# Moving the outer left sums of layer 0 to VectorE, ordering a logarithm behind a copy, and taking the last quad's inner sums from one quad earlier, in a two-layer graph kernel

## The chip, the cores and the metric

The kernel runs on one core of one Trainium2 chip. The metric is the device time of one execution in microseconds (us). All data are 32-bit floats. TensorE multiplies matrices, VectorE, ScalarE and GpSimd do the elementwise work, and the queues of SyncE, GpSimd and ScalarE start the transfers. In the lines of the profile these are PE (with PEld for its weight loads), DVE, ACT, POOL and SP.

## The reference

There are 128 graphs of 128 nodes with 512 features. Each of two layers normalises the features, applies a ReLU, runs a graph layer and adds the result to its input.

```python
# layer 0
h = maximum(layernorm(x), 0)
Xw = h @ Wv + bv
e = leaky_relu((Xw @ aw[:d])[:, None, :] + (Xw @ aw[d:])[:, :, None] + ab, 0.2)
a = adj * exp(e)
T = a / (sum(a, -1) + 1e-12)
x1 = x + relu(h @ Wk[0] + bk[0] + T @ h @ Wk[1] + bk[1] + T @ T @ h @ Wk[2] + bk[2])
# layer 1
h2 = maximum(layernorm(x1), 0)
q, k = split(h2 @ Wqk)
w = sum(q * (adj @ (k * mask)), -1) * mask / sqrt(512)
out = x1 + softmax(w, over the nodes)[:, :, None] * (h2 @ Wv1)
```

## The kernel before, in words

**Pairs and quads.** Layer 0 walks over 64 pairs of graphs, `for p in range(NP)`. Layer 1 walks over 32 quads, each two pairs, `q` from 0 to `NQ - 1`. All large products are done by a seven-product scheme of the Strassen-Winograd kind: the operands are cut into blocks, some sums of blocks are formed beforehand (the left sums of the activations, the right sums of the weights), and seven products replace eight. The results are chained through four PSUM banks `a`, `b`, `c`, `e`: after product 1 into `a`, ScalarE copies `a` to `b`; after product 6 has accumulated into `b`, ScalarE copies `b` to `c` (line 380, the value called U2 in Winograd's scheme); product 7 accumulates into `c`; ScalarE copies that to a buffer `s` (line 384); product 4 accumulates into `c` again. So product 7 waits for the copy of line 380, and product 4 for the copy of line 384. TensorE takes its instructions in the order written.

**One pair of layer 0.** The loop body for pair p runs: the attention matrix of pair p (`attention`, lines 454 to 473: scores z, an exponential, a row sum, the normalised matrix t, and beside it the transposed adjacency aT, scaled by the node mask on ScalarE in line 472); the products `y10` of pair p in the banks set1, with the transposes of t after product 6; `for_layer1(p - 1)`; the small products `inner` and `outer` with t; the sum with x in `outer` (line 526, VectorE); the products `y2` of pair p + 2 in the banks set2; two copies that seed the banks of the next `y10` (lines 486 and 490, after line 526); and `norm2(p)`, the layer norm of the result for layer 1. `norm0(p + 3)` and `begin(p + 2)` (norm, transposes in line 336 and left sums in lines 352 to 355 of later pairs) run in the course of `y10`.

**A layer norm.** `statistics` takes mean and variance on VectorE (lines 280 and 281), then a logarithm and an exponential on ScalarE (lines 285 and 286, the inverse root), five small VectorE instructions, and `norm_relu` applies the result with two large ScalarE instructions (line 304). The result goes to DRAM and comes back by 32x32 blocks, so that VectorE can transpose it.

**The outer left sums.** Layer 1 uses the seven-product scheme twice, one inside the other. `for_layer1(p)` transposes four blocks of a pair (line 410). After every second pair it forms the four outer left sums of the quad (lines 418, 419, 421, 422) and writes them to DRAM in two transfers of 1024 KB (lines 420 and 423). These sums are done by GpSimd for all quads but the last, which VectorE does.

**One quad of layer 1.** Two rounds of seven products run in step in the two sets of banks. Before the products, the inner left sums of each factor are formed from the outer ones, four VectorE instructions for the first four factors (called EARLY) and four for the other three (LATE: 3, 7, 4). The first round of an ordinary quad uses the factors 1, 5, 2, 6, the second 3, 7, 4. The last quad has another order: its first round uses 1, 6 and 2, 7, so it needs a LATE factor from its second product on. `scores` forms the row scores of the quad before (lines listed as `junk<-agg,wscale,c`), `spread_scores` sends them through DRAM to all partitions (`pwd`, `pw`), and `peaks` takes their maximum when they are back, ahead of the softmax.

**What sets the order.** A scheduler lays out each engine's instructions by priority (the order in which they are written) and by when it expects their inputs. `behind(what, op, ...)` fixes an order on top of it: `op` comes after the instruction `done[what]` on the engine that both run on. It adds nothing where the two run on different engines: `done["warm"]` is a matmul, so it holds back nothing on ScalarE. In layer 1 the orders are written out by hand: `dve`, `act`, `pool` and `sync` put each instruction behind the one before.

Of the kernel before, what the change touches and what calls it, by code (L numbers as in the profile page):

```python
# [8 lines left out]
FP = mybir.dt.float32  # L9
# [6 lines left out]
def kernel(  # L16
# [25 lines left out]
    nc = tc.nc  # L42
    B, N, D = x.shape
    K = wk.shape[0]
    P = 128
# [52 lines left out]
    def load_x(p, queue=nc.sync):  # L98
        xg[p] = loads.tile([P, G, D], FP, name="xg")
        queue.dma_start(xg[p], x[p * G:(p + 1) * G].rearrange("b n d -> n b d"))  # L100
# [78 lines left out]
    for dst, w in weights0:  # L179
        rows(dst, w, range(HC))  # L180

# [93 lines left out]
    def statistics(src):  # L275
# [9 lines left out]
        nc.scalar.activation(r[:, 0], var, AF.Ln, bias=eps)  # L285
# [73 lines left out]
    def strassen(banks, left, right, s, first, ends, steps={}, gate="warm"):  # L359
# [20 lines left out]
        nc.scalar.copy(c, b)  # L380
# [20 lines left out]
    def for_layer1(p):  # L401
# [10 lines left out]
        if second:  # L412
            fv = FW.pop(q).rearrange("p o j k n -> p o (j k n)")
            fd = FD[q].rearrange("p o j k n -> p o (j k n)")
            at = {o: fv[:, i] for o, i in SLOT.items()}

            engine, queue = (nc.gpsimd, nc.gpsimd) if q + 1 < NQ else (nc.vector, nc.sync)
            engine.tensor_add(at[5], fv[:, L21], at[4])
            engine.tensor_sub(at[6], at[5], at[1])
            queue.dma_start(fd[:, :4].rearrange("p o n -> p (o n)"), fv[:, :4].rearrange("p o n -> p (o n)"))  # L420
            engine.tensor_sub(at[3], at[2], at[6])
            engine.tensor_sub(at[7], at[1], fv[:, L21])  # L422
            queue.dma_start(fd[:, 4:].rearrange("p o n -> p (o n)"), fv[:, 4:].rearrange("p o n -> p (o n)"))
# [25 lines left out]
    def attention(p):  # L449
# [20 lines left out]
        for j in range(G):  # L470
            b = p * G + j
            nc.scalar.activation(aT[:, j, :], aT[:, j, :], AF.Copy, scale=maskT[:, b:b + 1])
# [57 lines left out]
    def norm2(p):  # L530

        HV2[p] = by_blocks(norm_relu(X1[p]), H2D[p])
# [45 lines left out]
    def inner_sums(q, factors):  # L578
# [3 lines left out]
        s = early.tile([P, 4, n, N], FP, name=f"in{first}")  # L582
# [37 lines left out]
    with tc.issue_after(done["hv"]):  # L620
        for p in (2, 3):
            load_x(p)
        load_adj(2)
        rows(rl[:, :, 1], wv1)

    for p in range(NP):
# [27 lines left out]
        behind("left", outer, p, z)  # L654
# [242 lines left out]
    for q in range(NQ - 1):  # L897
# [29 lines left out]
        if q > 0:  # L927
# [6 lines left out]
                     6: [lambda: scale(prior, 0, 1)]}  # L934
        together(one_round(q, set1, (3, 7), s1, adding_ends(lambda i, j: c[:, 0::3, i, j],
# [17 lines left out]
    for step in inner_sums(q, LATE):  # L953
        step()
# [113 lines left out]
```

## Time and profile before

The time before is 2357.18 us, the median of three runs (2349.5 to 2360.67). The profiled execution spans 2351.3 us. Layer 0 takes the first 1545 us or so, layer 1 the rest.

| stretch of the profile, us | PE busy | DVE busy | ACT busy | POOL busy |
|---|---|---|---|---|
| 0 to 100 (start of layer 0) | 85.12 | 52.80 | 39.39 | 20.22 |
| 300 to 600 (layer 0) | 286.60 | 195.89 | 151.35 | 86.28 |
| 900 to 1200 (layer 0) | 294.56 | 202.37 | 157.93 | 90.26 |
| 2000 to 2300 (layer 1) | 296.33 | 242.52 | 185.54 | 161.60 |
| 2300 to 2352 (end) | 32.89 | 36.48 | 21.67 | 11.07 |

A line of the timeline gives the start, the duration, the engine, the line of the kernel, the operation, the tiles written and read with their shapes, and how many instructions were merged (x4). Brackets give the idle time of that engine just before, and what released it. A line of the waits gives who waited for whom, the sum, the number of times and the longest, in us. A line of the stretches gives the busy time and the number of merged instructions of each engine, then TensorE's granted clock, the share of the DMA engines and the rate.

### The profile page before, as it was taken

The page shows a single profiled execution, that of the slowest core. Times are in us where ns is not written, and L with a number is a line of the kernel's source. Part 1 is how long each engine was busy: PE and PEld are TensorE (multiplying, and loading weights), DVE is VectorE, ACT ScalarE, POOL GpSimd, SP SyncE. Part 2 cuts the span into 40 slices and gives each one's busy share as a digit, 9 for nine tenths or more (in the row PEclk, how much of TensorE's full clock was granted, in tenths as well). Part 3 has the DMA queues.
Part 4 walks back from the last instruction along what each step waited for, and adds up shares of the span by engine and source line. Part 5 has one row for each costly group of instructions (what it writes and reads, how often), then busy time and mean ns, then how long its engine had stood idle before and what let it go on. Part 6 is the DMA issues. An engine that isn't in the chain of part 4 may idle for free.

```text
span 2351.3 us, 28892 instructions
## 1 busy us (share of the span) xinstructions
PE 2259.5 (96%) x8227; PEld 1541.8 (66%) x8227; DVE 1669.9 (71%) x4342; ACT 1262.1 (54%) x2932; POOL 847.4 (36%) x911
## 2 busy tenths in 40 slices
PE   8899999999999999999999999999999999999996
PEld 5565555656656566565665656578877878888785
DVE  5576665767667676676766667578877788888786
ACT  3444444555555455555555555446656666666564
POOL 2132222322322232232232223245545555555552
PEclk9999999999999999999999999999999999999998
DMA  7577686666676666666667666668787888888786
GB/s 212 154 233 231 203 248 197 216 216 209 194 235 201 199 228 201 206 211 215 205 205 224 198 198 225 203 240 238 225 226 228 223 239 233 222 238 239 219 233 166
DMA packets 343502, 507.77 MB, mean 216 GB/s; under 512 B 33178, under 2 KB 198426, under 8 KB 326958
## 3 DMA queue, kind: packets, MB, share of 16 engines
q1 hardware_dynamic: 302060, 382.40, 51.8%
q0 software_dynamic: 40992, 123.00, 19.7%
q8 instruction: 65, 1.06, 0.2%
q14 instruction: 95, 0.78, 0.1%
q10 hardware_dynamic: 290, 0.53, 0.1%
HBM read 289.62 MB, written 216.18 MB: 215 GB/s over the span
## 4 chain that ended last, share of the span: by engine, by line
PE 64%; DVE 16%; DMA 11%; ACT 4%; issue 3%; POOL 1%; SPq 1%; DVEq 0%; ACTq 0%
PE c L90 19%; PE a L90 18%; PE b L90 17%; PE e L90 10%; DMA pw<-pwd 3%; DVE junk L553 3%; DMA xg<-in_x_dram 2%; DVE x L526 2%; DVE st L280 2%; DMA pwd<-pwt 2%; ACT h L304 1%; DVE c L553 1%; DMA h2d<-h 1%; DVE s L553 1%; DVE in L553 1%
## 5 line engine op out<-in xcount | busy, mean ns | idle before, releaser
L553 POOL TENSOR_TENSOR c<-s,c 128x512 f32<-128x512 f32 (+1 forms) x186 | 199.9, 1089 | 370.4 <-DVE s L553 365.6
L110 POOL DMA_DIRECT2D agb<-in_adj_dram x256 | 150.3, 592 | 431.5 <-DVE aT L468 331.8
L90 PE MATMUL a<-r,x 128*128 128x512 f32 x512 | 246.4, 604 | 0.8 <-ACT a L486 0.5
L553 DVE SCALAR_TENSOR_TENSOR junk<-agg,wscale,c 128x512 f32<-128x512 f32 x128 | 197.6, 1543 | 31.7 <-POOL c L553 25.8
L90 PE MATMUL b<-rw,in 128*128 128x256 f32 x896 | 217.2, 382 | 0.9 <-ACT b L553 0.9
L90 PEld LDWEIGHTS b<-rw,in 128*128 128x128 f32 x896 | 172.0, 192 | 25.1 <-ACT b L553 1.3
L85 DVE TENSOR_TENSOR e<-e,s 128x512 f32<-128x512 f32 x64 | 44.7, 699 | 184.9 <-ACT s L384 184.9
L553 POOL TENSOR_TENSOR c<-c 128x1024 f32<-128x1024 f32 x62 | 159.5, 2573 | 2.8 <-DVE c L553 0.4
L90 PEld LDWEIGHTS a<-r,x 128*128 128x128 f32 x512 | 94.3, 195 | 68.2 <-issue 63.8
L90 PE MATMUL a<-w,x 128*128 128x257 f32 x512 | 131.9, 380 | 2.8 <-DVE z L454 2.8
L90 PE MATMUL b<-t,sx 128*128 128x512 f32 x256 | 124.3, 609 | 9.3 <-ACT b L376 9.3
L90 PE MATMUL b<-w,sx 128*128 128x257 f32 x512 | 132.1, 380 | 0.8 <-ACT b L376 0.6
L553 ACT ACTIVATE c<-c,wcol 128x512 f32<-128x512 f32 x124 | 86.2, 720 | 79.6 <-DVE wcol L553 79.6
L422 POOL TENSOR_TENSOR fw<-fw 128x512 f32<-128x512 f32 x31 | 39.1, 1263 | 247.7 <-DVE fw L410 247.7
L280 DVE BATCH_NORM_STATS2 st<-xg 128x6 f32<-128x512 f32 x128 | 82.1, 683 | 64.4 <-DMA xg<-in_x_dram 64.4
L90 PE MATMUL c<-t,x 128*128 128x512 f32 x256 | 120.9, 595 | 4.3 <-ACT s L384 4.3
L90 PE MATMUL c<-rw,in 128*128 128x256 f32 x448 | 110.1, 385 | 13.3 <-ACT c L553 13.1
L376 ACT COPY b<-a 128x257 f32<-128x257 f32 (+1 forms) x128 | 59.4, 464 | 116.5 <-PE a L90 116.3
L90 PE MATMUL e<-t,sx 128*128 128x512 f32 x256 | 120.3, 592 | 0.0
L90 PE MATMUL c<-t,sx 128*128 128x512 f32 x256 | 120.3, 592 | 0.0
L90 PE MATMUL b<-r,sx 128*128 128x512 f32 x256 | 120.3, 592 | 0.0
L90 PE MATMUL e<-rw,in 128*128 128x256 f32 x448 | 108.5, 381 | 5.8 <-DVE in L553 5.5
(247 smaller groups left out, 5351.3 us busy)
## 6 DMA issues: line engine op xcount, KB each, us to landing
fd<-fw POOLq DMA_DIRECT2D x62, 1024.0 KB, 6.6
x1d<-x SPq DMA_DIRECT2D x64, 512.0 KB, 2.8
h2d<-h SPq DMA_DIRECT2D x64, 512.0 KB, 4.8
hv<-h2d SPq DMA_DIRECT2D x256, 128.0 KB, 3.5
f<-fd SPq DMA_DIRECT2D x32, 1024.0 KB, 9.6
xg<-in_x_dram SPq DMA_DIRECT2D x63, 512.0 KB, 5.1
hd<-h SPq DMA_DIRECT2D x63, 512.0 KB, 3.1
hv<-hd SPq DMA_DIRECT2D x252, 128.0 KB, 2.9
```

The costliest lines, as they stand in the source:

```text
L85: return op(*args, **how)
L90: done["mm"] = op(*args, **how).ins
L110: nc.gpsimd.dma_start(agb[p][c * S32:(c + 1) * S32].rearrange("p g q i -> p (g q) i"), v[c])
L280: nc.vector.bn_stats(st, src[:, j, :])
L304: nc.scalar.activation(to, at, AF.Relu, bias=rs[:, 1, j:j + 1], scale=rs[:, 0, j:j + 1])
L376: nc.scalar.copy(b, a)
L422: engine.tensor_sub(at[7], at[1], fv[:, L21])
L526: done["x1"] = nc.vector.scalar_tensor_tensor(hb[:, j, at], bank[:, HD:], 0.0, xs[:, j, at], OP.max, OP.add).ins
L553: done[engine] = op(*args, **how).ins
```

## The change

There are four edits.

1. The four outer left sums of every quad are done by VectorE, right behind the transposes whose results they add, and before the sums with x (line 526), which are put behind the last of them. The transfers stay on GpSimd's queue.
2. The logarithm of `norm2` (line 285) is put behind the copy of U2 (line 380) in the `y2` just issued, the copy of U2 behind the copy of line 85, and the scaling of the transposed adjacency (line 472) behind the exponential of line 456.
3. The four LATE inner sums of the last quad move from that quad's start into the second round of the quad before, in buffers of their own.
4. The input of pair 2 is loaded at the start, behind the weights, and no longer after pair 1's first norm.

```diff
     for dst, w in weights0:
         rows(dst, w, range(HC))
+    load_x(2)
...
-    def statistics(src):
+    def statistics(src, gate="warm"):
...
-        nc.scalar.activation(r[:, 0], var, AF.Ln, bias=eps)
+        behind(gate, nc.scalar.activation, r[:, 0], var, AF.Ln, bias=eps)
...
         product(b, 6)
-        nc.scalar.copy(c, b)
+        done["u2"] = behind("s", nc.scalar.copy, c, b).ins
...
-            engine, queue = (nc.gpsimd, nc.gpsimd) if q + 1 < NQ else (nc.vector, nc.sync)
-            engine.tensor_add(at[5], fv[:, L21], at[4])
-            engine.tensor_sub(at[6], at[5], at[1])
+            queue = nc.gpsimd if q + 1 < NQ else nc.sync
+            nc.vector.tensor_add(at[5], fv[:, L21], at[4])
+            nc.vector.tensor_sub(at[6], at[5], at[1])
             queue.dma_start(fd[:, :4].rearrange("p o n -> p (o n)"), fv[:, :4].rearrange("p o n -> p (o n)"))
-            engine.tensor_sub(at[3], at[2], at[6])
-            engine.tensor_sub(at[7], at[1], fv[:, L21])
+            nc.vector.tensor_sub(at[7], at[1], fv[:, L21])
+            done["c12"] = nc.vector.tensor_sub(at[3], at[2], at[6]).ins
...
-            nc.scalar.activation(aT[:, j, :], aT[:, j, :], AF.Copy, scale=maskT[:, b:b + 1])
+            behind("z", nc.scalar.activation, aT[:, j, :], aT[:, j, :], AF.Copy, scale=maskT[:, b:b + 1])
...
-        HV2[p] = by_blocks(norm_relu(X1[p]), H2D[p])
+        HV2[p] = by_blocks(norm_relu(X1[p], rs=statistics(X1[p], "u2")), H2D[p])
...
-    def inner_sums(q, factors):
+    def inner_sums(q, factors, space=None):
...
-        s = early.tile([P, 4, n, N], FP, name=f"in{first}")
+        s = (space or early).tile([P, 4, n, N], FP, name=f"in{first}")
...
-        for p in (2, 3):
-            load_x(p)
+        load_x(3)
...
-        behind("left", outer, p, z)
+        behind("c12" if p else "left", outer, p, z)
...
+        if q == NQ - 2:
+            sums = inner_sums(NQ - 1, LATE, back[3])
+            hooks[2], hooks[3] = hooks[2] + sums[:2], hooks[3] + sums[2:]
...
-    for step in inner_sums(q, LATE):
-        step()
```

## The prediction

> **What bounds the kernel now.** I read the stretches first, then the waits of TensorE, then the timeline where these waits lie. A settled stretch of layer 0 and one of layer 1:
>
> ```profile
> 600.00:900.00 300.00, 294.25 (x989) 182.19 (x988) 205.16 (x663) 158.44 (x377) 87.16 (x121) 1.00 0.68 214
> ...
> 2000.00:2300.00 300.00, 296.33 (x1266) 240.89 (x1265) 242.52 (x419) 185.54 (x419) 161.60 (x120) 0.99 0.82 232
> ```
>
> TensorE (first number) is busy 98% of both stages, so it sets the pace, and only what makes it wait can be won: under 6 us in 300. TensorE's waits in 600 to 900 say what that is:
>
> ```profile
> PE c L90 <- ACT c L380: 5.1, 7, 0.7
> ...
> PE c L90 <- ACT s L384: 0.7, 1, 0.7
> ```
>
> Seven times in 300 us, once in two pairs (a double pair takes 45.0 us). Over the whole trace this wait is 17.8 us in 24 times. The timeline of such a pair:
>
> ```profile
> 600.13 1.28 POOL L421 TENSOR_TENSOR fw<-fw 128x512 f32<-128x512 f32 x1
> ...
> 600.40 1.10 DVE L454 TENSOR_SCALAR z<-pz,y,cz 128x128 f32<-128x128 f32 x1
> ...
> 601.63 0.29 ACT L285 ACTIVATE r<-mv,eps 128x2 f32<-128x2 f32 x1 [0.74 <-DVE mv L281]
> ...
> 602.22 0.40 ACT L472 ACTIVATE aT<-aT,maskT 128x128 f32<-128x128 f32 x1
> ...
> 602.52 0.36 ACT L380 COPY c<-b 128x257 f32<-128x257 f32 x1
> ...
> 602.94 1.13 PE L90 MATMUL c<-w,sx 128*128 128x257 f32 x4 [0.72 <-ACT c L380]
> ...
> 623.29 0.32 DVE L454 TENSOR_SCALAR z<-pz,y,cz 128x128 f32<-128x128 f32 x1
> ```
>
> The z instruction takes 1.10 us while GpSimd adds, and 0.32 in the next pair, where GpSimd has no sums. The variance behind it comes late, ScalarE sits 0.74 us before the logarithm, and U2's copy, queued behind logarithm, exponential and mask scaling, starts at 602.52, though product 6 was over at 601.35. TensorE stands for 0.72 us.
>
> Before 400 us the loss is larger. An early pair with sums:
>
> ```profile
> 169.97 0.36 ACT L380 COPY c<-b 128x257 f32<-128x257 f32 x1 [0.49 <-PE b L90]
> ...
> 171.80 0.30 ACT L285 ACTIVATE r<-mv,eps 128x2 f32<-128x2 f32 x1 [1.47 <-DVE mv L281]
> ...
> 172.36 0.36 ACT L384 COPY s<-c 128x257 f32<-128x257 f32 x1
> ...
> 173.34 1.71 DVE L454 TENSOR_SCALAR z<-pz,y,cz 128x128 f32<-128x128 f32 x1
> ...
> 177.35 1.52 ACT L304 ACTIVATE h<-x,rs 128x512 f32<-128x512 f32 x2
> ...
> 179.99 3.43 PE L90 MATMUL b<-t,sx 128*128 128x512 f32 x4 [2.65 <-ACT b L376]
> ```
>
> VectorE is held up by GpSimd's adds (two sums of `prepare` took 1.38 and 1.40 us, in the pair after 0.39 each), so z and norm are late, ScalarE's copy of line 376 is queued behind them, and TensorE waits 2.65 us and runs at half clock afterwards (3.43 us for what takes 1.88). Between 100 and 395 us such waits add up to 19.5 us (0.79, 2.65, 2.65, 3.80, 1.18, 0.92, 2.39, 3.83, 1.32).
>
> At the start the second pair waits for the input of pair 2, at the end the last quad for its LATE sums:
>
> ```profile
> 51.10 1.29 DVE L280 BATCH_NORM_STATS2 st<-xg 128x6 f32<-128x512 f32 x2 [4.06 <-DMA xg<-in_x_dram]
> ...
> 68.69 1.13 PE L90 MATMUL a<-w,x 128*128 128x257 f32 x4 [2.82 <-DVE z L454]
> ```
>
> ```profile
> 2312.61 1.22 PE L90 MATMUL e<-rw,in 128*128 128x256 f32 x2 [5.48 <-DVE in L553]
> ...
> 2313.62 3.62 PE L90 MATMUL b<-rw,in 128*128 128x256 f32 x8
> ...
> 2322.74 0.68 DVE L553 TENSOR_REDUCE peak<-pw 128x4 f32<-128x512 f32 x1
> ...
> 2327.71 0.70 PE L90 MATMUL a<-rw,f 128*128 128x256 f32 x2
> ```
>
> **What the Trainium skill says.** "SBUF — State Buffer", section "Who interferes with whom": VectorE and GpSimd share a port pair under an exclusive lock; a VectorE instruction with two SBUF inputs, or a `tensor_scalar` in its two-port mode, waits for the whole of a GpSimd instruction that reads SBUF. The trace agrees: 1.10 and 1.71 us against 0.32. "TensorE: Matmul & The Clock Gate", section "What's actually happening": after an idle window of about 3.4 us the clock halves until TensorE has been busy as long. The trace agrees in kind: after 5.5 us of idling eight matmuls took 3.62 us, against 1.89 in other rounds; here 2.65 us was enough too, and 0.72 never was.
>
> **The sums on VectorE.** They leave GpSimd (31 quads of four, 1.26 to 1.28 us each), which has time enough, so the time saved there is worth nothing by itself. On VectorE the same shape took 0.65 to 0.68 us in the last quad, started every 0.57 to 0.60: 4 x 0.6, and 0.1 for a dependence, make 2.5 us a quad, 78 us over layer 0, where VectorE is busy 68%. In a settled pair the transposes start at 594.23; 1.36 us later come the sums, so line 526 can start at 598.1, and started at 597.49. It is 0.6 us late, and behind it queue the seed copies: 598.55 and 599.07, free at 599.65, when the next copy (line 376) started before: 599.65. So the delay just fits, and TensorE sees at most 0.1. Later VectorE has 4.00 us of idle time (before 592.57) to catch up in. The two 1024 KB transfers start 2 to 3 us earlier on a queue that nothing waits for here. What is won: z costs 0.32 for 1.10.
>
> **Logarithm behind U2's copy.** No instruction is added. The copy can start at 601.4 and ends at 601.8, before TensorE is through with product 2 (602.22): the 0.72 us is gone. New is that logarithm, exponential, five small VectorE instructions and the two large ones of line 304 queue behind the copy. In the pairs without sums the logarithm moves from 623.73 to about 624.6 and line 304 from 625.78 to 626.6. Their result goes to DRAM and has 10 us until it is transposed. The mask scaling behind the exponential gives the exponential its place 0.4 us sooner; the scaled matrix is first read in layer 1.
> Sum for the settled part: 24 x 0.72 = 17.3 us, less 24 x 0.1 for the late seeds and about 1 us for other small waits: -14.
>
> **Early pairs.** VectorE gets back 1.0 + 1.0 + 1.4 = 3.4 us of blocking for 2.5 us of sums, but the sums and the transposes must now come before line 526. There the transposes stood behind it (167.72 against 166.08); VectorE was idle for 2.28 us before it, so line 526 comes between 1.6 us (4 - 2.3, if the blocks are there) and 4 us later. That puts up to 1 us on U2's chain and takes some 2 us off the chain z, norm, line 376. I take half of the 19.5 us: -9; the bounds are 0 and -19.5 with up to 1.5 us of slow clock for each of four waits.
>
> **Input of pair 2.** The load is on the queue behind the weights, with the DMA engines full from 10 to 30 us, so it lands at 30 us or so instead of 51. What goes before it isn't moved. The 4.06 us wait of VectorE goes, TensorE's 2.82 us with it, as TensorE was free at 65.9. With 0.5 us for the exponential of pair 0 that now precedes the mask scaling: -3. Bounds: 0 and -6.
>
> **LATE sums.** Four instructions of 0.55 us leave the gap in which TensorE stood 5.48 us and lost another 2.3 us to half clock. That is not won in full. The end hangs on the softmax of the quad before: its scores started at 2307.03, left VectorE at 2311.9, their maximum came at 2322.74, and agg, scaling and the last rounds follow from there on ScalarE and VectorE. In the quad before, VectorE is busy without a gap from 2298.4 to 2306.2, and the 2.1 us of added sums push those scores back by as much. The scores were back at about 2318.7 (issue 2314.12, 4.6 us to land); with 2.1 us more the maximum can run at 2320.9 instead of 2322.74: -1.9. TensorE would be done with its round at 2317 and idle until 2325.8, so its next products run at half clock for a time, as at 2313.62: +2. Sum 0, bounds -3 and +3.
>
> **Total:** -14 - 9 - 3 + 0 = -26 us; 2357.2 - 26 = 2331, rounded to 2332.
>
> **The rivals.**
> - *The copy of line 384 takes the place of line 380 (25%).* It and line 304 become ready almost together: the copy 1.0 to 1.1 us after U2's copy (product 7), line 304 after 0.33 + 0.24 + five times 0.2 = 1.6. If the scheduler puts line 304 first, as it does in the settled pairs now, product 4 waits: about 0.55 us in the pairs with sums, 0.7 in the others, where nothing was lost. Per double pair that is 0.53 us worse than now, 24 times: +12.7; with -3 at the start and nothing won early, 2367, slower. For it: the present order. Against it: in the early pairs, where the logarithm runs behind U2's copy by chance, the copy at 172.36 is ahead of line 304 at 177.35.
> - *The early pairs stay as they are (20%).* The late line 526 holds back seeds and line 376, and eats what VectorE wins: 2357.2 - 14 - 3 = 2340.
> - *All waits of layer 0 go (10%).* 17.8 + 19.5 + 4 x 1.5 + 3 = 46 us: 2311. For it: every early wait goes back to a VectorE that GpSimd holds up. Against it: half of them are in pairs without sums.
>
> **How the numbers follow.** The forecast has 45%. It, the second rival in three cases of four, and the third are faster by over 11.8 us: 0.70. The first rival's 2367 lies near the bound (2369), so its 25% are split: 0.13 slower and 0.12 same, and the rest of the second makes same 0.17. The range from 2312 to 2362 leaves out the greater part of the first rival and half of the third.
>
> **What would show it.** Right: no GpSimd adds in layer 0, z at 0.32 us in all pairs, no wait for line 380, a double pair of 44.3 us instead of 45.0, seeds at most 0.7 us later, statistics of pair 2 before 48 us, no wait at 2312 but the maximum hardly earlier. Wrong: waits for line 384 twice in a double pair; waits of TensorE for line 376 or 486 behind a late line 526, above all where VectorE waits for the blocks from DRAM ahead of the transposes; or a longer first 30 us, where the extra 512 KB would hold up the weights.

## The result, and the profile after

The changed kernel takes 2332.24 us in the median (2326.47 to 2337.88), beside 2358.8 us of the kernel before in the same comparison: a ratio of 0.9895, with a 95% interval from 0.9857 to 0.9933, or 26.6 us less. The prediction said 2332 us. The sum lies close, closer than these few runs can tell. The table shows that it is right for partly wrong reasons. It gives the time between marks of the two profiles, where a mark is the start of the sums with x (line 526, after the change 527) of a pair.

| stretch | before, us | after, us | difference | predicted |
|---|---|---|---|---|
| start to pair 1 | 98.8 | 98.6 | -0.2 | -3 |
| pair 1 to 13 (early) | 295.8 | 285.2 | -10.6 | -9 |
| pair 13 to 63 (settled) | 1125.1 | 1110.5 | -14.6 | -14 |
| pair 63 to the end (layer 1) | 831.6 | 839.1 | +7.5 | 0 |

The differences add up to -17.9 us and not to -26.6, because each profile is one run: the two profiled runs took 2353.3 and 2335.1 us, beside medians of 2358.8 and 2332.2. So the table tells where time went, to some microseconds, and not the whole amount.

The stretches of the changed kernel, with TensorE's busy time first, answer to those shown of before:

```profile
600.00:900.00 300.00, 298.03 (x1015) 188.69 (x1013) 212.26 (x700) 159.12 (x383) 54.58 (x94) 1.00 0.70 214
2000.00:2300.00 300.00, 292.47 (x1252) 236.70 (x1250) 239.95 (x411) 179.51 (x405) 156.80 (x117) 1.00 0.79 222
```

In layer 0 TensorE is busy for 298.03 of 300 us instead of 294.25, and GpSimd for 54.58 instead of 87.16. In layer 1 it is busy for 292.47 instead of 296.33 us, but this stretch lies 18 us nearer to the end of the shorter run, and from 1700 to 2000 us it is the other way round (292.85 before, 295.70 after), so nothing is read from it. The waits of TensorE over the whole trace:

```profile
PE c L90 <- ACT c L554: 16.9, 14, 4.8
PE c L90 <- ACT s L385: 14.5, 21, 2.4
PE a L90 <- ACT agg L554: 9.4, 1, 9.4
...
PE a L90 <- ACT a L487: 3.5, 1, 3.5
...
PE c L90 <- ACT c L85: 2.1, 5, 0.7
```

The wait for U2's copy (now listed as `ACT c L85`, since each ordered instruction carries the line of `behind`) went from 17.8 us to 2.1. Others grew or came: 3.5 us for a seed copy (0.5 before), 9.4 us for a copy at the end, and 14.5 us for the copy of line 385 (384 before), which stood so in the kernel before:

```profile
PE c L90 <- ACT s L384: 10.3, 12, 2.4
```

Between 390 and 1500 us this last wait grew from 4.3 to 10.3 us. The timeline of a settled pair with sums shows what the change was to bring:

```profile
651.42 0.32 DVE L455 TENSOR_SCALAR z<-pz,y,cz 128x128 f32<-128x128 f32 x1
...
652.40 0.36 ACT L85 COPY c<-b 128x257 f32<-128x257 f32 x1 [0.49 <-PE b L90]
652.67 0.30 ACT L85 ACTIVATE r<-mv,eps 128x2 f32<-128x2 f32 x1
...
654.13 0.38 ACT L385 COPY s<-c 128x257 f32<-128x257 f32 x1
```

The z instruction takes 0.32 us where it took 1.10, and the logarithm (652.67) stands behind U2's copy (652.40). But now a pair nearly 300 us later:

```profile
921.60 0.38 SPq L326 DMA_DIRECT2D h2d<-h  x1
...
922.03 0.46 SPq L100 DMA_DIRECT2D xg<-in_x_dram  x1
...
928.63 1.29 DVE L281 BATCH_NORM_STATS2 st<-xg 128x6 f32<-128x512 f32 x2 [3.69 <-DMA xg<-in_x_dram]
...
931.72 1.52 ACT L305 ACTIVATE h<-xg,rs 128x512 f32<-128x512 f32 x2 [1.02 <-DVE rs L293]
933.14 0.56 ACT L385 COPY s<-c 128x512 f32<-128x512 f32 x1
...
933.76 3.05 PE L90 MATMUL c<-t,x 128*128 128x512 f32 x4 [2.07 <-ACT s L385]
```

SyncE's queue writes h of the second norm to DRAM at 921.60, as soon as line 305 is through, and only then starts the load of x for a later pair (922.03), although the buffer of that load was free at 915.6. VectorE stands for 3.69 us until x is there, the first norm of that pair comes late on ScalarE (931.72), the copy of line 385 is queued behind it (933.14), and TensorE waits 2.07 us for product 4 and goes on at half clock (3.05 us for what takes 1.88). The chain of waits says the same of the whole run, as shares of the span by engine and line. The kernel before:

```profile
PE c L90 19%; PE a L90 18%; PE b L90 17%; PE e L90 10%; DMA pw<-pwd 3%; DVE junk L553 3%; DMA xg<-in_x_dram 2%; DVE x L526 2%; DVE st L280 2%; DMA pwd<-pwt 2%; ACT h L304 1%; DVE c L553 1%; DMA h2d<-h 1%; DVE s L553 1%; DVE in L553 1%
```

The changed kernel:

```profile
PE c L90 16%; PE a L90 15%; PE b L90 14%; DMA xg<-in_x_dram 9%; PE e L90 9%; ACT h L305 4%; DMA pw<-pwd 3%; DMA pwd<-pwt 3%; DVE junk L554 3%; DVE st L281 2%; DVE c L554 1%; DVE s L554 1%; DMA h2d<-h 1%; DVE wcol L554 1%; DVE fw L411 1%
```

The load of x grew from 2% to 9% of the chain, line 304/305 from 1% to 4%, at TensorE's cost. The timeline at the start of the changed kernel:

```profile
50.02 1.28 DVE L281 BATCH_NORM_STATS2 st<-xg 128x6 f32<-128x512 f32 x2
...
70.34 1.50 PE L90 MATMUL a<-w,x 128*128 128x257 f32 x4 [3.11 <-DVE z L455]
```

The statistics of pair 2 start without a wait for x, but TensorE still waits for z. The timeline in the last quad:

```profile
2288.87 4.06 DVE L554 SCALAR_TENSOR_TENSOR junk<-agg,wscale,c 128x512 f32<-128x512 f32 x1 [0.79 <-POOL c L554]
...
2304.67 0.69 DVE L554 TENSOR_REDUCE peak<-pw 128x4 f32<-128x512 f32 x1 [8.02 <-DMA pw<-pwd]
...
2309.65 1.22 PE L90 MATMUL a<-rw,f 128*128 128x256 f32 x2 [9.40 <-ACT agg L554]
```

The last quad has no gap at its LATE sums any more, but TensorE waits 9.40 us for the copy of the aggregates instead, and goes on at half clock (1.22 us for what takes 0.70).

### The profile page after: what moved, and what is told of

Its sections match the earlier page's. It is cut to its first block, busy times and chain, and to the rows that moved or that the text cites. A ratio compares the mean times of both kernels' runs of the same rounds, so it can differ in the third digit from the quotient of the medians.

```text
span 2333.3 us, 28894 instructions
## 1 busy us (share of the span) xinstructions
PE 2247.4 (96%) x8227; PEld 1549.4 (66%) x8227; DVE 1679.4 (72%) x4466; ACT 1254.2 (54%) x2932; POOL 690.4 (30%) x787
## 4 chain that ended last, share of the span: by engine, by line
PE 55%; DMA 18%; DVE 15%; ACT 8%; issue 2%; SPq 1%; POOL 1%; DVEq 0%; POOLq 0%; ACTq 0%
PE c L90 16%; PE a L90 15%; PE b L90 14%; DMA xg<-in_x_dram 9%; PE e L90 9%; ACT h L305 4%; DMA pw<-pwd 3%; DMA pwd<-pwt 3%; DVE junk L554 3%; DVE st L281 2%; DVE c L554 1%; DVE s L554 1%; DMA h2d<-h 1%; DVE wcol L554 1%; DVE fw L411 1%
## 5 line engine op out<-in xcount | busy, mean ns | idle before, releaser
L554 DVE SCALAR_TENSOR_TENSOR junk<-agg,wscale,c 128x512 f32<-128x512 f32 x128 | 198.0, 1547 | 30.9 <-POOL c L554 25.6
L85 DVE TENSOR_TENSOR e<-e,s 128x512 f32<-128x512 f32 x64 | 44.7, 698 | 119.9 <-ACT s L385 119.9
L305 ACT ACTIVATE h<-xg,rs 128x512 f32<-128x512 f32 x128 | 97.2, 806 | 56.8 <-DVE rs L293 56.7
L90 PE MATMUL a<-rw,f 128*128 128x256 f32 x448 | 108.9, 382 | 9.7 <-ACT agg L554 9.4
```

The costliest lines, as they stand in the source:

```text
L85: return op(*args, **how)
L90: done["mm"] = op(*args, **how).ins
L305: nc.scalar.activation(to, at, AF.Relu, bias=rs[:, 1, j:j + 1], scale=rs[:, 0, j:j + 1])
L554: done[engine] = op(*args, **how).ins
```

## The experiments

Times are medians. Each group shares its runs of the kernel before, and the difference is taken to that. The kernel before has 2348.5 to 2350.7 us in the later groups, with 9 to 41 runs each, and 2358.8 in the four runs of the first, so the first row is the least certain one.

| version | time, us | before, us | ratio (95%) | difference |
|---|---|---|---|---|
| whole change | 2332.2 | 2358.8 | 0.9895 (0.9857 to 0.9933) | -26.6 |
| edit 1 alone (sums) | 2308.8 | 2350.7 | 0.9824 (0.9811 to 0.9837) | -41.9 |
| edit 2 alone (order) | 2357.5 | 2350.7 | 1.0038 (1.0020 to 1.0056) | +6.8 |
| edit 3 alone (LATE) | 2358.1 | 2350.7 | 1.0032 (1.0021 to 1.0042) | +7.4 |
| edit 4 alone (x of pair 2) | 2348.6 | 2350.7 | 0.9991 (0.9982 to 1.0000) | -2.0 |
| without edit 2 | 2312.9 | 2350.3 | 0.9835 (0.9812 to 0.9857) | -37.4 |
| without edit 3 | 2316.8 | 2350.3 | 0.9854 (0.9833 to 0.9875) | -33.5 |
| load of x ahead of h | 2345.1 | 2350.3 | 0.9975 (0.9967 to 0.9984) | -5.2 |
| without the logarithm's order | 2322.4 | 2349.2 | 0.9878 (0.9855 to 0.9900) | -26.8 |
| load of x on GpSimd's queue | 2301.1 | 2349.2 | 0.9788 (0.9765 to 0.9811) | -48.1 |
| edits 1, 4, tail split | 2300.6 | 2350.3 | 0.9784 (0.9760 to 0.9808) | -49.7 |
| the same, last block on VectorE | 2295.0 | 2349.2 | 0.9769 (0.9743 to 0.9795) | -54.2 |
| the same, load on GpSimd's queue | 2290.7 | 2348.5 | 0.9757 (0.9741 to 0.9773) | -57.8 |

And the stretches of the profiles, in us (one profile each; the start, left out here, lies between 91 and 99 us without regard to the edits; kernels whose layer 0 is the same differ by up to 3.4 us from pair 1 to 13 and by up to 2.2 us from 13 to 63, and kernels whose layer 1 is the same by up to 7.8 us from pair 63 to the end):

| version | pair 1 to 13 | pair 13 to 63 | pair 63 to the end |
|---|---|---|---|
| before | 295.8 | 1125.1 | 831.6 |
| whole change | 285.2 | 1110.5 | 839.1 |
| edit 1 alone | 280.4 | 1102.0 | 829.6 |
| edit 2 alone | 293.2 | 1127.4 | 833.2 |
| edit 3 alone | 293.0 | 1125.8 | 840.3 |
| without edit 2 | 281.8 | 1099.8 | 832.5 |
| without edit 3 | 284.6 | 1109.5 | 827.5 |
| load of x ahead of h | 286.2 | 1126.6 | 836.1 |
| without the logarithm's order | 286.8 | 1106.4 | 836.2 |
| load of x on GpSimd's queue | 267.6 | 1100.2 | 835.2 |
| edits 1, 4, tail split | 278.7 | 1100.0 | 825.3 |
| the same, last block on VectorE | 278.4 | 1101.7 | 818.4 |
| the same, load on GpSimd's queue | 268.9 | 1107.3 | 821.1 |

### Each edit alone

Edit 1 alone:

```diff
-            engine, queue = (nc.gpsimd, nc.gpsimd) if q + 1 < NQ else (nc.vector, nc.sync)
+            queue = nc.gpsimd if q + 1 < NQ else nc.sync
...
-            engine.tensor_add(at[5], fv[:, L21], at[4])
+            nc.vector.tensor_add(at[5], fv[:, L21], at[4])
...
-        behind("left", outer, p, z)
+        behind("c12" if p else "left", outer, p, z)
```

> The kernel before with edit 1 alone (outer left sums on VectorE, and line 526 behind them). Theory A: the settled wait of 0.72 us in every second pair has two causes in a row, VectorE held up by GpSimd's sums (which makes the variance late) and U2's copy queued behind the logarithm on ScalarE. Taking either away removes it. So this edit alone wins the settled 24 x 0.72 = 17 us and the 10 us of the early pairs: ratio 0.988 to 0.991, and no z instruction over 0.4 us. Theory B: the place of the copy on ScalarE is what counts, and sums on VectorE only make line 526 late: ratio 0.999 to 1.006.

It won 41.9 us, more than the whole change and more than either theory said. (Line 526 no longer waits behind the left sums with this edit. In the kernel before these started 7 us or more ahead of it from pair 1 on, so that order had held nothing back.) TensorE's waits in the settled part (390 to 1500 us), with edit 1 alone:

```profile
PE a L90 <- ACT a L486: 2.7, 1, 2.7
PE c L90 <- ACT c L380: 2.2, 6, 0.6
...
PE c L90 <- ACT s L384: 0.4, 1, 0.4
```

The wait for U2's copy is 2.2 us instead of 17.8, though the logarithm is as free as before. The group of VectorE's z instructions before (busy time in us and mean in ns behind the bar):

```profile
L454 DVE TENSOR_SCALAR z<-pz,y,cz 128x128 f32<-128x128 f32 x124 | 63.3, 511 | 0.0
```

The groups of z and of one of the four sums with edit 1 alone:

```profile
L454 DVE TENSOR_SCALAR z<-pz,y,cz 128x128 f32<-128x128 f32 x124 | 39.6, 320 | 0.0
...
L422 DVE TENSOR_TENSOR fw<-fw 128x512 f32<-128x512 f32 x32 | 22.1, 692 | 1.1
```

The mean of z falls from 511 to 320 ns, and the four sums cost 0.65 to 0.69 us each on VectorE, as estimated.

Edit 2 alone:

```diff
-        nc.scalar.copy(c, b)
+        done["u2"] = behind("s", nc.scalar.copy, c, b).ins
...
-            nc.scalar.activation(aT[:, j, :], aT[:, j, :], AF.Copy, scale=maskT[:, b:b + 1])
+            behind("z", nc.scalar.activation, aT[:, j, :], aT[:, j, :], AF.Copy, scale=maskT[:, b:b + 1])
...
-        HV2[p] = by_blocks(norm_relu(X1[p]), H2D[p])
+        HV2[p] = by_blocks(norm_relu(X1[p], rs=statistics(X1[p], "u2")), H2D[p])
```

> The kernel before with edit 2 alone (logarithm behind U2's copy, that copy behind line 85, mask scaling behind the exponential). Theory A: the settled 17 us go, the waits before 400 us stay, since they come from a VectorE that GpSimd holds up: ratio 0.992 to 0.994, first thirteen pairs as before. Theory B (a wait takes the place of the one removed): the copy of line 384 or the norm behind it comes late while z is still held up, and the ratio is 0.998 to 1.005.

It made the kernel 6.8 us slower; its profile is of the fastest of seven runs and shows less of that. In the settled part the waits for U2's copy went (24 times, 17.8 us), and TensorE waited for the copy of line 384 in their place: 24 times in the narrow product `c<-w,x`, 7.5 us in sum, and 12 times in the wide product `c<-t,x`, 20.7 us, after which it twice ran at half clock. One of the twelve, from the timeline of edit 2 alone:

```profile
503.49 0.38 SPq L528 DMA_DIRECT2D x1d<-x  x1
...
508.63 1.52 ACT L304 ACTIVATE h<-x,rs 128x512 f32<-128x512 f32 x2 [0.24 <-DVE rs L292]
...
510.17 0.38 SPq L325 DMA_DIRECT2D h2d<-h  x1
...
510.60 1.30 SPq L100 DMA_DIRECT2D xg<-in_x_dram  x1
...
518.59 1.29 DVE L280 BATCH_NORM_STATS2 st<-xg 128x6 f32<-128x512 f32 x2 [5.08 <-DMA xg<-in_x_dram]
...
523.11 0.56 ACT L384 COPY s<-c 128x512 f32<-128x512 f32 x1
...
523.72 3.52 PE L90 MATMUL c<-t,x 128*128 128x512 f32 x4 [3.63 <-ACT s L384]
```

The load of x (510.60) stands behind the write of h (510.17), which waits for line 304 (508.63). Already before the change this was so in 14 of 47 settled pairs, with the load 6.2 us in the mean behind the write of x1 (503.49 here); with edit 2 it is 6.8 us. In the whole change it is 23 of 46 pairs at 6.4 us, without edit 2 21 of 46 at 5.9 us. So edit 2 makes a load that was already at its limit half a microsecond later. The Trainium skill says why such an issue cannot be overtaken ("DMA: Bandwidth & Descriptors", section "Anatomy of one DMA — SWDGE (gpsimd) path"): DMA engines do not wait on semaphores; the wait happens on the issuing sequencer, before dispatch. The trace agrees: the load's buffer is free after 503.4, and it starts 0.43 us after the write it does not depend on.

Edit 3 alone:

```diff
+        if q == NQ - 2:
+            sums = inner_sums(NQ - 1, LATE, back[3])
+            hooks[2], hooks[3] = hooks[2] + sums[:2], hooks[3] + sums[2:]
...
-    for step in inner_sums(q, LATE):
-        step()
```

> The kernel before with edit 3 alone (LATE sums of the last quad one quad sooner). Theory A: the end hangs on the scores that go through DRAM; the sums put them back by 2 us, and the 5.5 us wait of TensorE only moves to a later place, where half clock follows too: +2 us, ratio 1.000 to 1.002. Theory B: TensorE's wait of 5.5 us and its half clock are on the path: -5 to -8 us, ratio 0.9966 to 0.998.

It cost 7.4 us, and the profiles show where. First, at the end: from the last maximum but one to the end of the run it is 57.4 to 58.5 us in the six kernels with edit 3, and 54.7 to 55.3 us in the five kernels that keep the tail of before: +2.9 us in the mean. The scores come 2 us later behind the added sums, as the prediction said, and TensorE, no longer held up earlier, waits 9.5 us for the copy of the aggregates and goes on at half clock. Second, at the start of layer 1, which the prediction did not look at: from pair 63 to the first maximum it is 49.5 to 52.2 us with edit 3 and 45.3 to 47.3 us in the eight kernels without, +4.1 us. The timeline of SyncE with edit 3 alone:

```profile
1541.41 0.34 SPq L423 DMA_DIRECT2D fd<-fw  x1
1546.98 0.37 SPq L553 DMA_DIRECT2D h<-h2d  x1
```

The same for the kernel before:

```profile
1545.14 0.38 SPq L553 DMA_DIRECT2D h<-h2d  x1
...
1547.47 0.33 SPq L420 DMA_DIRECT2D fd<-fw  x1
```

Before, the first load of h2 for the second quad goes out ahead of the transfers of the last left sums; with edit 3 it goes out 5.6 us after the second of them. The waits of SyncE around the first quads of the whole change name the releaser:

```profile
SPq L554 <- DMA pwd<-pwt: 7.1, 1, 7.1
SPq L554 <- DMA fd<-fw: 4.7, 2, 2.4
```

This wait for `fd<-fw` is there in all six kernels with edit 3 and in none of the others, where SyncE waits 1.2 to 1.5 us for a transpose into `fw` instead. The new buffer of the sums takes 6 KB of each partition (4 x 3 x 128 numbers of 4 bytes) in the pool `back[3]`, which also holds that h2; so presumably a tile of that pool came to lie where `fw` of layer 0 is still being read. The wait is measured, this reason for it is argued. The scores' round trip behind these loads then takes longer (7.1 us from `pwd` to `pw`, 3.3 us in the version without edit 3), and TensorE waits for the softmax.

Edit 4 alone:

```diff
+    load_x(2)
...
-        for p in (2, 3):
-            load_x(p)
+        load_x(3)
```

> The kernel before with edit 4 alone (input of pair 2 loaded at the start). Theory A, as predicted: VectorE's 4.06 us wait at 51 us and TensorE's 2.82 us at 68.7 us go, nothing before is later: -3 us, ratio 0.9987. Theory B, from the trace of the changed kernel, where the products with the first weights began at 35 us instead of 30: the extra 512 KB hold up the weights while the DMA engines are full, and the 5 us lost there outweigh what is won: +1 to +3 us, ratio 1.0004 to 1.0013. Either way the start of the first pair and of the second in the trace tell.

It won 2.0 us, at the border of what can be told. In its timeline the statistics of pair 2 start at 46.20 with no wait, and TensorE's wait for z at pair 1's products is 1.01 us instead of 2.82. VectorE's wait is gone in all ten kernels with edit 4; but TensorE's wait for z is 1.0 us in only three of them and 2.7 to 3.4 us in the other seven, beside 2.7 to 4.6 us in the four kernels without. One of the seven, without edit 2, shows VectorE standing for the next thing there, h on its way back from DRAM (1.55 us before its transpose at 63.11). So the wait that edit 4 was made for went, and a gain from it is not shown.

### Each of two edits taken out

Without edit 2 (edits 1, 3 and 4) and without edit 3 (edits 1, 2 and 4):

> The change without the order of the logarithm (edits 1, 3 and 4). If the single edits add up, edit 2 costs 6.8 us in this company too, or more, since the sums on VectorE already take away the waits that edit 2 was made for: 2350.7 - 41.9 + 7.4 - 2.0 = 2314, between 2310 and 2319; pairs 13 to 63 take 1102 us as with the sums alone. If edit 2 only costs where the sums stay on GpSimd (rival), the run stays within 3 us of the whole change, 2330 to 2334, and pairs 13 to 63 take 1110.

> The change with the LATE sums left where they were (edits 1, 2 and 4). If edit 3 costs 7 us at the end for its own sake (scores of the quad before start 2 us later, behind an addition of GpSimd, and TensorE stands for 9 us ahead of the last quad's matrix of aggregates): 2325, between 2322 and 2328; from pair 63 to the end 831 instead of 839 us, and no wait of 9 us for that copy. If layer 1's loss in the whole change has another cause (rival: loads that come late in both), no more than 2 us is won: 2330 to 2334.

Both are faster than the whole change: by 10.8 us and by 6.9 us, going by the differences from before. By the medians themselves it is 19.3 and 15.4 us, because of the slower runs of the kernel before in the first group, and the interval of the whole change is wide (9 us to either side). So the sign is clear, the size is not, and the profiles have to bear it out. (Without edit 3 the time is under the expected 2322 to 2328.) Without edit 2, pairs 13 to 63 take 10.7 us less (1099.8 against 1110.5) and pairs 1 to 13 3.4 us less. By the profiles edit 2 costs more there in company than alone (2.3 us), since edit 1 has already taken the waits it was made for. Without edit 3, the two places named above are back at 46.2 us (50.2 in the whole change) and 54.7 us (57.4), 6.7 us in sum. The four single differences add up to -29.7 us, beside -26.6 us measured.

### Is it the load of x?

If edit 2 costs time through the load that is queued behind h, moving the load must give the time back. The first try puts the load first on the same queue:

```diff
-        queue.dma_start(xg[p], x[p * G:(p + 1) * G].rearrange("b n d -> n b d"))
+        done["xl"] = queue.dma_start(xg[p], x[p * G:(p + 1) * G].rearrange("b n d -> n b d")).ins
...
-        hd = dram.tile([G, P, D], FP, name="hd") if hd is None else hd
-        nc.sync.dma_start(hd.rearrange("g n d -> n g d"), h)
+        ahead, hd = (ExitStack(), dram.tile([G, P, D], FP, name="hd")) if hd is None else (tc.issue_after(done["xl"]), hd)
+        with ahead: nc.sync.dma_start(hd.rearrange("g n d -> n g d"), h)
...
-        norm2(p)
         if p + 4 < NP:
             load_x(p + 4)
+        norm2(p)
```

> The whole change, but the transfer of h to DRAM (line 326) is held behind the load of a later pair's x on SyncE's queue, so that this load no longer waits for the second norm. If edit 2 costs time because that load is queued behind the late h (theory): SyncE no longer waits with loads behind line 326, VectorE's statistics do not wait for x, TensorE's waits for the copy of line 385 in the wide product fall from 1.0 to 2.4 us to 0.7 or none, pairs 13 to 63 fall from 1110 to 1103 us or so, and the time to about 2325 (2321 to 2329). If the loss comes from the logarithm and the norm standing later on ScalarE themselves (rival), the waits for line 385 stay and the time is 2330 to 2336.

Half of this came true. The load is out 0.4 us after x1, VectorE's wait for x is all but gone (3.4 us, once), and TensorE's waits for line 385 fell from 14.5 to 1.5 us. But the time is 2345 us, for the scheduler now lays out ScalarE differently. The timeline of such a pair:

```profile
908.88 1.50 ACT L305 ACTIVATE h<-x,rs 128x512 f32<-128x512 f32 x2
...
910.29 0.39 ACT L85 ACTIVATE aT<-aT,maskT 128x128 f32<-128x128 f32 x1
...
910.58 0.58 ACT L377 COPY b<-a 128x512 f32<-128x512 f32 x1
...
911.21 1.98 PE L90 MATMUL b<-t,sx 128*128 128x512 f32 x4 [1.35 <-ACT b L377]
```

Line 305 of the second norm and a mask scaling stand ahead of the copy of line 377 (910.58), whose input was ready at 908.1, and TensorE waits 1.35 us, once in every double pair: 33 us in 25 times. The two 0.8 us instructions of line 305, moved late by edit 2, have to fit between two copies that TensorE waits for, and here they don't. So the time of this run decides nothing; its waits fit the load as the cause of those for line 385.

The second try leaves the order of writing alone and uses another queue:

```diff
-            load_x(p + 4)
+            load_x(p + 4, nc.gpsimd)
```

> The whole change, with the load of a later pair's x on GpSimd's queue in layer 0, where since edit 1 no sum is in its way and no transfer of h stands ahead of it; the order of the logarithm stays. If edit 2 costs time through this load alone (theory), VectorE's statistics never wait for x by microseconds, TensorE's waits of 1 to 2.4 us for line 385 in the wide product go without a wait for line 377 in their place, pairs 13 to 63 take 1102 us (1100 to 1105) and not 1110, and the time is 2320 to 2326. If a norm that comes later costs ScalarE's copies their turn whatever the load does (rival), waits for line 377 or 385 stay at 10 us or more in sum, and the time is 2330 to 2345.

2301.1 us, 21 us better than the whole change by the differences from before, and better than the expected 2320 to 2326. The settled part takes 1100.2 us, as the theory said. The waits of 1 to 2.4 us for line 385 in the wide product are gone, but for one of 0.2 us; VectorE still waits for x in the settled part, 22.8 us in 21 times, 2.0 us at most. What stays is a wait of 0.4 us in the narrow product, once in most double pairs. The waits for lines 377 and 385 come to 11.8 us together, which is the sign that the rival named. But it isn't edit 2 that brings it, for it is there as well in the last version below, which has the load on GpSimd's queue and no edit 2. TensorE's waits for this copy with edit 2:

```profile
PE c L90 <- ACT s L385: 9.7, 23, 1.1
```

And without:

```profile
PE c L90 <- ACT s L385: 9.5, 24, 2.0
```

In the pairs read of both, line 385's copy stands between the two instructions of line 305 of the second norm. The early pairs, for which nothing was expected, take 267.6 us instead of 285.2. The waits of VectorE for transfers between 100 and 390 us tell why. Of x in the kernel before:

```profile
DVE st L280 <- DMA xg<-in_x_dram: 25.0, 8, 5.6
```

Of x in the changed kernel:

```profile
DVE st L281 <- DMA xg<-in_x_dram: 20.1, 7, 5.2
```

All that is left for transfers with the load on GpSimd's queue:

```profile
DVE x L337 <- DMA hv<-hd: 5.4, 2, 3.3
...
DVE fw L411 <- DMA hv<-h2d: 1.4, 1, 1.4
```

The wait for x is gone. In the early pair that the prediction shows, the load goes out at 179.32, right behind the write of h (178.90), 11.5 us after the write of x1 (167.83).

The logarithm's order taken out, the two small orders left:

```diff
-        HV2[p] = by_blocks(norm_relu(X1[p], rs=statistics(X1[p], "u2")), H2D[p])
+        HV2[p] = by_blocks(norm_relu(X1[p], rs=statistics(X1[p], "warm")), H2D[p])
```

> The whole change with the two small orders of edit 2 (U2's copy behind the copy of line 85, the mask scaling behind the exponential), but the logarithm of the second norm free. If the order of the logarithm is what costs (theory), this run equals the change without edit 2 (ratio to before 0.9835, here 2310 to 2317), with few transfers of h ahead of the load of x on SyncE's queue. If the mask scaling or the copy's order costs (rival), it stays at 2325 to 2333.

At -26.8 us beside before it is not told apart from the whole change (-26.6). In its profile the settled part is 4 us shorter (1106.4), of the 10.7 us that edit 2 costs there. So the logarithm alone is not what costs: the theory in this form fell. Which of the two small orders costs the rest was not run. Nor does this rest come through the load of x: only 11 of 46 loads stand behind the write of h, VectorE waits for x no less than in the whole change (66.7 us in 35 times, beside 58.4 in 35), and TensorE doesn't wait for line 385 in the wide product in that part. It waits 4.8 us in 12 times for that line in the narrow product, and 3.6 us in 8 times for U2's copy. (The list of SyncE's waits puts 187 us of the write of h, in 40 times, down to the ordered mask scaling. That name is wrong: in all 40 the write goes out 0.02 to 0.03 us after line 305 is over, and 0.27 us before the scaling is.)

### A version that beats both

Edits 1 and 4, with the tail repaired in another way: two LATE sums ahead of the scores, two behind their transpose, and the addition of the last block in the last quad on VectorE:

```diff
     begin_quad(q)
+    sums = inner_sums(q, LATE)
+    for step in sums[:2]:
+        step()
     catch_up(q)
...
-    for step in inner_sums(q, LATE):
+    for step in sums[2:]:
         step()
-    last_block(prior)
+    dve(nc.vector.tensor_add, outer(prior, 1), outer(prior, 3), outer(prior, 1))
```

> Edits 1 and 4, and in the last quad two of the four LATE sums ahead of the scores of the quad before, two behind the transpose that sends them off, and the addition of the last block of that quad on VectorE behind them and not on GpSimd. If the scores' instruction takes 4 us because GpSimd's addition of 128x1024 holds VectorE up, it takes 0.7 to 0.8 us here; the maximum comes 2 us sooner than with the sums alone, TensorE's wait of 6.2 us for the sums falls under 1.5 us, and the time is 2.6 to 6 us under the sums alone (2308.8): 2303 to 2306. If the 4 us are the instruction's own (rival: it waits for something else, as the copy of its input), it stays at 4 us, the maximum comes 1.1 us later, and the time is 2306 to 2310.

2300.6 us, some 8 us better than edit 1 alone (with edit 4 among them, and the change of the tail not taken apart) and better than expected. The timeline of the scores with edit 1 alone, where GpSimd adds beside them:

```profile
2262.72 4.04 DVE L553 SCALAR_TENSOR_TENSOR junk<-agg,wscale,c 128x512 f32<-128x512 f32 x1 [0.79 <-POOL c L553]
2263.40 2.79 POOL L553 TENSOR_TENSOR c<-c 128x1024 f32<-128x1024 f32 x1
```

The same in this version, where it doesn't:

```profile
2258.26 0.74 DVE L554 SCALAR_TENSOR_TENSOR junk<-agg,wscale,c 128x512 f32<-128x512 f32 x1
```

0.74 us instead of 4.04: the instruction is listed as running until 0.6 us after the end of GpSimd's addition, although its listed start is 0.7 us earlier than that of the addition. This fits the lock of the shared port pair ("SBUF — State Buffer", section "Who interferes with whom"), which the prediction cited for z and did not look for here: an instruction of VectorE with two inputs in SBUF stands still for the whole of GpSimd's 2.8 us. Why it stood still though it is listed as the first to start, the trace doesn't tell. From the last maximum but one to the end it is 52.2 us instead of 54.7.

In ordinary quads the scores stand behind the same addition. With it on VectorE in all of them:

```diff
-        pool(nc.gpsimd.tensor_add, outer(q, 1), outer(q, 3), outer(q, 1))
+        dve(nc.vector.tensor_add, outer(q, 1), outer(q, 3), outer(q, 1))
```

> The version with the repaired tail (edits 1 and 4; two LATE sums ahead of the scores, two behind), with the addition of the last block (128x1024) on VectorE in all quads. If the first scores instruction takes 4.05 us in each quad because it stands behind GpSimd's 2.8 us addition, it takes 0.75 us in all quads, the probabilities are back 3.3 us sooner less the 1.2 us of the added instruction elsewhere, TensorE's waits of 11 us for ScalarE's copy in layer 1 fall under 5, and the time is 4 to 9 us under 2300.6: 2292 to 2297. If these waits come from the transfers (rival), they stay and the time is within 2 us of 2300.6, or higher, as VectorE has the addition on top.

The group of the scores with edit 1 alone (busy time, and mean in ns):

```profile
L553 DVE SCALAR_TENSOR_TENSOR junk<-agg,wscale,c 128x512 f32<-128x512 f32 x128 | 198.0, 1547 | 31.1 <-POOL c L553 25.8 <-ACT agg L553 0.8
```

The same group in this version:

```profile
L554 DVE SCALAR_TENSOR_TENSOR junk<-agg,wscale,c 128x512 f32<-128x512 f32 x128 | 97.6, 762 | 30.7 <-POOL c L554 25.1 <-ACT agg L554 0.8 <-ACT ej L554 0.5
```

2295.0 us, within the expectation. A quarter of the 128 instructions, one in each quad, had been blocked (4.0 to 4.1 us in 29 of 32, 2.3 to 3.4 in three), and one is now, with 2.2 us (762 ns in the mean of all for 1547). TensorE's wait for ScalarE's copy in layer 1 fell from 11.1 to 5.2 us, and pair 63 to the end from 825.3 to 818.4 us. Last, the same with the load of x on GpSimd's queue:

> Edits 1 and 4 without edit 2, the repaired tail with the last block's addition on VectorE, and the load of a later pair's x on GpSimd's queue in layer 0. Its layer 0 differs from that of the whole change with the same queue by edit 2 alone. If the gain from pair 1 to 13 comes from the load (theory), this stretch takes 268 us (265 to 272) as there, and not 278; if the order of the logarithm is worth something once the load is out of its way (rival), pairs 1 to 63 take 10 us or more above the 1367.8 us of that run; by the theory they differ by less than 5. Time: 2295.0 - 10.8 - 1.5 = 2283 by the theory (2277 to 2288), 2290 or more by the rival.

2290.7 us, the fastest version, and above the expected 2283. The early pairs do take 268.9 us. But the settled part takes 1107.3 us, beside 1100.2 us with the same queue and edit 2: over pairs 1 to 63 it is 1376.2 against 1367.8 us, 8.4 us, between what the theory and the rival said. So the order of edit 2 seems to be worth some microseconds once the load is out of its way, by one profile of each: the double pair is 44.4 us in this version and 44.2 us with edit 2. In TensorE's narrow products 7 and 4 this shows as starts 0.1 us late: 111 times in this version, 9.6 us in sum, and 23 times with edit 2. Edit 2 on top of this fastest version was not run. Nor did the load's move win here what it won with edit 2: the settled part is 5.6 us longer than with the load on SyncE's queue (1101.7), and what the version gains lies in the early pairs (268.9 for 278.4).

## Why the prediction was right, and where not

**Settled part, -14 predicted, -14.6 measured: right sum, wrong source.** The prediction gave the 17.3 us to the copy of U2 and the order that puts the logarithm behind it. Edit 1 alone wins 23.1 us here (1125.1 to 1102.0), edit 2 alone loses 2.3, and edit 2 loses 10.7 on top of the rest. What held the copy up was the variance that came late behind a blocked z, as the prediction itself read from the timeline at 601.63; once z takes 0.32 us, the logarithm (908.51 to 908.80 in one pair with edit 1 alone) is over before product 6 (909.02). The exponential and a mask scaling still stand ahead of the copy there and cost product 7 0.1 us. The double pair takes 44.4 us in the mean with the whole change (1110.5/25), as foretold (44.3), and 44.1 with edit 1 alone. That edit 1 wins more than the 17.8 us listed is for the most part a matter of counting. From start to start of TensorE's matmuls, the 24 products behind the copy came 0.89 us late each, 21.7 us in sum. The view of waits counts from the listed end of the matmul before, 0.38 us after its start, where the next one of a product follows after 0.22 us; so the term 24 x 0.72 was itself too small. By the same count all delays in this part fall from 42.7 to 19.7 us.

**The failed step: "Their result goes to DRAM and has 10 us until it is transposed."** It followed the data of the second norm, and these mostly have the time: between 390 and 1500 us VectorE waits for them 12.6 us in 18 times, and 6.2 us in 9 times before. It did not ask what is queued behind the write of h on SyncE: the load of x, which VectorE, then the first norm, then the copy of line 385 wait for. With the load moved away from that queue, the loss is gone: on SyncE's queue the settled part takes 1099.8 to 1102.0 us without edit 2 and 1109.5 to 1110.5 with it, on GpSimd's queue 1107.3 without and 1100.2 with it. So what edit 2 is worth turns with the place of the load. That the two small orders without the logarithm's still cost some microseconds on SyncE's queue (1106.4 us) is not explained by the load, and stays open. The first rival had the same gap. Its "product 4 waits" came about with edit 2 alone, 24 times in the narrow product, at 0.31 us and not 0.55 to 0.7; but the greater part (20.7 of 28.2 us) is in the wide product and comes through the load.

**Early pairs, -9 predicted, -10.6 measured.** VectorE held up by GpSimd was named as the cause of all 19.5 us. Edit 1 alone brings 15.4 us. The late load of x is a second cause: VectorE waited 25.0 us for it before, in a view that the prediction did not use, and moving it to another queue wins another 17.6 us on top of the whole change and 9.5 us in the last version. All in all the stretch is then 28.2 us shorter than before, more than all the waits with their slow clock that the prediction counted (25.5 us). The late line 526 did no harm that shows; in the one of these pairs that was read the seed copies stand behind line 377 (172.71 against 169.84 in the changed kernel), and the stretch did not stay as it was, so the second rival didn't come.

**Input of pair 2, -3 predicted, -2.0 measured with edit 4 alone.** The wait of VectorE went. That TensorE's 2.82 us would go with it is the step that doesn't hold: 1.8 us went with edit 4 alone, but with the whole change the wait for z was 3.11 us, and it is 2.7 us or more in seven of the ten kernels with edit 4. In the run of the whole change the first products started at 35.07 instead of 29.89; in the nine other kernels with edit 4 they start between 29.56 and 30.67, so it is not shown that the load delays the weights.

**LATE sums, 0 predicted, +7 measured.** The terms at the end were right in kind: the scores 2 us later, TensorE idle and at half clock. The gain of -1.9 for an earlier maximum did not come: the distance from scores to maximum is 15.7 us before and 15.8 after, because the load `pw` went out 5.34 us after `pwd` (2294.00 to 2299.34) and not 1.98 us after it as before (2312.14 to 2314.12). What this round trip shared the transfers with was not tested. That leaves +2.9. The other +4.1 lie where the new wait for `fd<-fw` is: "buffers of their own" were costed at nothing, and presumably took a place that layer 0 was still using.

**The total** was right since the missed loss of edit 2 (10.8) and of edit 3 (7) stood against a gain of edit 1 (41.9) that was 19 us larger than what the prediction gave both stretches of layer 0 (23). That these errors are of one size is luck, and their sizes are known to some microseconds only. The third rival, "all waits of layer 0 go", with 46 us, is close to what edit 1 alone did.

## What to carry to other kernels

Before an instruction is moved later, follow not only its result but what is queued behind the transfer that carries it: an unrelated load on the same queue inherits the delay. When several edits of a change go for the same wait, test which of them removes it; the others may then only cost. And a new buffer is an edit of the memory plan: look for new waits where the pools of two stages meet, far from the place of the edit.

## What was not expected of the hardware

- One addition of 2.8 us on GpSimd cost VectorE 3.3 us in nearly every quad of layer 1 (4.0 to 4.1 us for an instruction of 0.75 in 29 of 32 quads).
- "TensorE: Matmul & The Clock Gate", section "What's actually happening", gives an idle window of about 3.4 us that runs freely. Here the clock halved after waits of 2.07 and 2.40 us (3.05 and 3.14 us for a product of 1.88), and did not after one of 3.54 us (1.98 us). In the kernel before, a wait of 2.65 us was followed by half clock at 179.99 and not at 228.99. So a single wait says little, as a freely running window would have it.
- "DMA: Bandwidth & Descriptors", section "Issuing engines are not separate DMA queues", says that starting transfers from several engines saves only the time of starting them. Here a load moved to GpSimd's queue (0.73 us to issue) saved 21 us with edit 2 in the kernel, because of what it no longer waits behind, and 3.6 us without (57.8 less than before instead of 54.2).
